# A graph-attention layer on one core: the row fetches of the sync engine leave, every tile is gathered, and more of the gathers wait for TensorE

## The chip, the cores and the metric

The kernel runs on one core of one Trainium2 chip. The metric is device time in microseconds (us): lower is better. A core has TensorE (PE in the profile, with its weight loads as PEld), VectorE (DVE), ScalarE (ACT), GpSimd (POOL) and the sync engine (SP), each with an instruction queue of its own, and 16 DMA engines that move data between HBM and the on-chip memory. The time before is 2110.27 us, the median of three runs (2109.47 to 2112.22).

## The reference

One graph-attention layer with a batch norm and a layer norm, on 12,500 nodes of 128 features (8 heads of 16) and 212,500 edges that are sorted by their target node:

```python
Q, K, V = (x @ WQ), (x @ WK), (x @ WV)            # each (N, 8, 16)
Eh = (edge_attr @ WE)                             # (E, 8, 16)
score = exp(clip((K[src] * Q[dst] / sqrt(16) * Eh).sum(-1), -5, 5))
wV = segment_sum(V[src] * score, dst)
Z  = segment_sum(score, dst)
h  = x + wV / (Z + 1e-6)
h  = (h - mean(h)) * rsqrt(var(h) + 1e-5) * gamma + beta    # over the nodes
out = layernorm(x + h)                                      # over the features
```

What matters here is `K[src]` and `V[src]`: for each edge a row of 256 floats (K and V side by side, 1 KB) has to come from a table, at an index that is data.

## The kernel before, in words

**Tiles and groups.** The edges are cut into T = 1661 tiles of 128. Four tiles make a unit (`U`; the last two units have 3 and 2), and two units make a group (`G` = 8 tiles; the last has 5), so there are NG = 208 groups. A unit's targets lie in a window of 64 nodes.

**The prelude.** It projects x with WK and WV (`table_rows`, L674) and writes the table `kvd` (12,500 rows of 1 KB) to HBM. Meanwhile GpSimd gathers rows of x itself for the first 8 groups (`nxg`), 64 tiles; their K and V are projected from those (`project`, L330), three groups in the prelude and five in the first iterations of the loop. `load_rest` (L166) issues loads from ACT's queue, among them two of `row_ids`, the indices for the row fetches below. `place(runs[0])` (L375) runs in the prelude too; the later runs are placed from iteration 20 on. `place` turns the targets' places within their window (`rel`) by TensorE and writes them as bf16 rows to `relT` in HBM, from where `load_rel` (L400, one group) and `load_quad` (L389, four groups) bring them back, broadcast over 64 partitions. `turned_onehot` (L532) compares them with the partition number.

**The loop.** Iteration g (L793) works on several groups at once, a stage apart. On TensorE, in this order: `add_x(g-3)` (L658), `q_mm(g+3)` (L544, matmul L546), `gather_sum(g-1)` (L629, matmuls L636), `turn_back(g+1)` (L580, L586) and `ehqe(g+2)` (L560, L565 and L573). On VectorE: `products(g)` (L591, K times the turned Q·E, L597), `both(g+1)` (L575), `scores(g)` (L603), small steps, `message(g)` (V times the weight, L621) and `onehot(g+1)`.

**The gathers.** From group 8 on, K and V of a group come by indirect DMAs that GpSimd issues, one of 128 rows for each tile (`gather`, L229, the instruction at L230), into one of nine slots of 8 tiles (slots 0 to 7, and slot 8 from the end of iteration 6). `message(g)` frees the slot of its group; `load_kv` (L284) then puts the gathers of the next group that has none into the list `queued`, and iteration g+1 issues them. From group 17 on, the slot that `message(g)` frees goes to group g+9. `pace(step)` (L241) makes the first gather of the list wait for a TensorE instruction, here `q_mm(g+3)`, from iteration 12 on; `issue()` sends the others without such a wait.

**The rows by the sync engine.** For every eighth group from 18 on (24 groups, `row_plan`, L58), the last tile isn't gathered. SP reads 16 indices in each iteration from 8 on and issues a DMA of one row of 1 KB for each (`fetch_rows`, L273, the DMA at L282), 3072 in all, into the tile `byrow`. So the table's gathers are 1573. In those groups `parts` (L270) splits the second `products` and the `message` in two, one piece for the fetched tile.

**The end.** After the last group come the batch norm's sums, the layer norm of 25 blocks and the output.

Of the kernel before, what the change touches and what calls it, by code (L numbers as in the profile page):

```python
# [9 lines left out]
BF16 = mybir.dt.bfloat16  # L10
U8 = mybir.dt.uint8
I32 = mybir.dt.int32
# [17 lines left out]
ROWS = P  # L30
FIRST_ROW = 8
ROW_LAG = 3
ROW_STREAMS = (("SP", 16),)
RQ = 4
# [22 lines left out]

def row_plan(sizes):  # L58


    full = sizes.count(U) // 2
    used, plan_ = set(), []
    for _, n in ROW_STREAMS:
        groups, end = [], 0
        while True:
            end += P
            g = FIRST_ROW + -(-end // n) - 1 + ROW_LAG
            while g in used:
                g += 1
            if g >= full:  # L70
                break
            used.add(g)
            groups.append(g)
        plan_.append(groups)
    return plan_


def row_groups(sizes):
    return [2 * g for groups in row_plan(sizes) for g in groups]


@with_exitstack
def gnn_kernel(
# [42 lines left out]
    kvd = dram.tile([N, 2 * P], F32, name="kvd")  # L126
    relT = dram.tile([T, P], BF16, name="relT")

# [37 lines left out]
    def load_rest():  # L166
        nc.scalar.dma_start(base_i, bass.AP(tensor=dstb.tensor, offset=dstb.offset, ap=[[0, P], [1, NW]]))
        nc.scalar.dma_start(rel_i[:, :cut], dst[:, :cut])
        for q, m, c, n, at in row_loads:
            nc.scalar.dma_start(row_ids[q % P:q % P + m, c:c + n], bass.AP(  # L170
                tensor=rsrc.tensor, offset=rsrc.offset + at, ap=[[n, m], [1, n]]))
        nc.scalar.dma_start(w_q, wq)
        nc.scalar.dma_start(w_e, we)
        nc.scalar.dma_start(srcs[:, nxg * G:cut], src[:, nxg * G:cut])
# [48 lines left out]
    def kv_view(g, t):  # L223
        SLOT[g] = t[0]
        v = t[1].rearrange("p (g d) -> p g d", d=2 * P)
        KV[g] = lambda a, b, c, n=P: (v[:, a:b, c:c + n] if g not in by_row or b < G else
                                      by_row[g][:, :, c:c + n])

# [20 lines left out]

    by_row, fill = {}, {}  # L250
    row_loads = []
    cols = ids = 0
    for (_, n), groups in zip(ROW_STREAMS, row_plan(usizes)):
        tot = len(groups) * P
        for q in range(-(-tot // n)):
            at = (q % P, cols + q // P * n, min(n, tot - q * n))
            fill.setdefault(FIRST_ROW + q, []).append(at + (groups, q * n))
        for q in range(0, tot // n, P):
            row_loads.append((q, min(P, tot // n - q), cols + q // P * n, n, ids + q * n))
        if tot % n:  # L260
            q = tot // n
            row_loads.append((q, 1, cols + q // P * n, tot % n, ids + q * n))
        cols += -(-tot // (P * n)) * n
        ids += tot
        by_row.update({g: None for g in groups})
    row_ids = consts.tile([P, cols], I32, name="row_ids")
    nc.vector.memset(row_ids, 0)
    kvb = kvd.bitcast(U8).rearrange("n d -> (n d)")

    def parts(g, a, b):  # L270
        return [(a, b - 1), (b - 1, b)] if g in by_row and b == G else [(a, b)]

    def fetch_rows(g):  # L273
        for p, c, n, groups, at in fill.get(g, []):
            _, offs = nc.values_load_multi_w_load_instructions(
                row_ids[p:p + 1, c:c + n], engines=(ET.SP,), min_val=0, max_val=(N - 1) * 8 * P,
                skip_runtime_bounds_check_because="node ids")
            for r, off in enumerate(offs, at):
                k = groups[r // P]
                if r % P == 0:  # L280
                    by_row[k] = late[0].tile([P, 1, 2 * P], F32, name="byrow", bufs=2)
                nc.sync.dma_start(by_row[k][r % P:r % P + 1, 0, :].bitcast(U8), kvb[ds(off, 8 * P)].unsqueeze(0))  # L282

    def load_kv():  # L284
        while free and pending and table[0]:
            g = pending.pop(0)
            i = free.pop(0)
            kv_view(g, (i, slot(i)))
            for j in range(sizes[g] - (g in by_row)):
                queued.append((gather, KV[g](j, j + 1, 0, 2 * P).rearrange("p a d -> p (a d)"), kvd,  # L290
                               starts[g] + j))
            if not steady[0]:
                issue()
# [81 lines left out]
    def place(r):  # L375
        nc.vector.tensor_copy(vw(rel, r), vw(rel_i, r))
        nc.vector.tensor_tensor(vw(rel, r), vw(rel, r), bc(base_f, r), op=OP.subtract)
        end = ustarts[r[0]] + (r[1] - r[0]) * r[2]
        for t in range(ustarts[r[0]], end, P):
            n = min(P, end - t)  # L380
            ps = spare_ps
            nc.tensor.transpose(ps[:n], rel[:, t:t + n], ident)
            row = wp.tile([P, P], BF16, name="relrow", bufs=2)
            nc.vector.tensor_copy(row[:n], ps[:n])
            nc.scalar.dma_start(relT[t:t + n, :], row[:n])

    RB = {}

    def load_quad(q):  # L389
        t = late[0].tile([P, RQ, U * P], BF16, name="rbq", bufs=2)  # L390
        for h in (0, 1):
            at = ustarts[2 * RQ * q + h] * P
            nc.sync.dma_start(t[h * WN:(h + 1) * WN], bass.AP(
                tensor=relT.tensor, offset=relT.offset + at, ap=[[0, WN], [G * P, RQ], [1, U * P]]))
        for k in range(RQ):
            RB[RQ * q + k] = t[:, k, :]

    quads = range(-(-2 * FIRST_ROW // RQ), sizes.count(G) // RQ)

    def load_rel(g):  # L400
# [3 lines left out]
        for h in (0, 1):  # L404
            t, n = ustarts[2 * g + h], usizes[2 * g + h]
            nc.sync.dma_start(RB[g][h * WN:(h + 1) * WN, :n * P],
                              bass.AP(tensor=relT.tensor, offset=relT.offset + t * P, ap=[[0, WN], [1, n * P]]))

# [151 lines left out]
    def ehqe(g):  # L560

        QE[g], WT[g] = [], []
        for a, b in halves(g):
            eh = psp.tile([P, U * P], F32, name="ps_e", bufs=2)[:, :(b - a) * P]
            nc.tensor.matmul(eh, w_e, EA[g][:, a:b, :].rearrange("p a b -> p (a b)"), start=True, stop=True)  # L565
            t = wp.tile([P, U * P], F32, name="wt", bufs=2)
# [3 lines left out]
        for k in range(3):  # L570
            for h, (a, b) in enumerate(halves(g)):
                r = slice(h * WN, (h + 1) * WN)
                nc.tensor.matmul(QE[g][h], Q3[g][r, k, :], OT[g][r, :(b - a) * P], start=(k == 0), stop=(k == 2))  # L573

    def both(g, h):  # L575
# [4 lines left out]
    def turn_back(g):  # L580

        PW[g] = []
        for h, (a, b) in enumerate(halves(g)):
            ps = turned()
            for j in range(b - a):
                nc.tensor.transpose(ps[:, j, :], WT[g][h][:, j * P:(j + 1) * P], ident)  # L586
            PW[g].append(ps)

    PR, SS, RZ = {}, {}, {}

    def products(g, hs=(0, 1)):  # L591
        if 0 in hs:
            PR[g] = wp.tile([P, G, P], F32, name="p", bufs=1)
        for i in hs:
            a, b = halves(g)[i]
            for c, d in parts(g, a, b):
                nc.vector.tensor_tensor(PR[g][:, c:d, :], KV[g](c, d, 0), PW[g][i][:, c - a:d - a, :], op=OP.mult)  # L597

# [16 lines left out]
    def message(g, h=None):  # L615
        if h is not None:
            ranges = parts(g, *halves(g)[h])
        else:
            ranges = halves(g) if g < nxg and g not in SLOT else parts(g, 0, sizes[g])
        for a, b in ranges:  # L620
# [8 lines left out]
    def gather_sum(g):  # L629
# [3 lines left out]
        for j in [*range(n - 1), *range(n, nt(g)), n - 1]:  # L633
            if g and j == n - 1:
                nc.tensor.matmul(AGG[g][0:1, :], carry[WN:, g - 1:g], OS[g - 1][WN:], start=False, stop=False)
            nc.tensor.matmul(AGG[g][WN if j >= n else 0:], OH[g][j], MSG[g][:, j, :], start=(j == 0),  # L636
                             stop=(j == n - 1))

# [154 lines left out]
    for g in range(NG - 2):  # L793
        within(load, g + 4)
        within(load_rel, g + 5)
        if (g + 6) % RQ == 0 and (g + 6) // RQ in quads:
            load_quad((g + 6) // RQ)
        fetch_rows(g)
        within(products, g)
        within(both_halves, g + 1)  # L800
        step = within(add_x, g - 3)
        step = within(q_mm, g + 3) or step
        if step is not None and queued and g >= FIRST_ROW + 4:
            pace(step)
        issue()
        within(gather_sum, g - 1)
        if g + 1 < nxg and g + 1 not in SLOT:
            for _ in project_main(g + 1):
                pass
        within(turn_back, g + 1)  # L810
        within(scores, g)
# [9 lines left out]
        within(turned_onehot, g + 3)  # L821
        within(ehqe, g + 2)
        within(q_mid, g + 3)
# [11 lines left out]
        if g == NG - 5:  # L835
            assert done >= set(range(NPRE))
            norm_first()
        if g == 4:
            nc.vector.tensor_scalar(row_ids, row_ids, 8 * P, None, op0=OP.mult)
        if g == FIRST_ROW - 1:  # L840
            tps.close()
            late.append(tps.enter_context(tc.tile_pool(name="late", bufs=1)))
        if g == FIRST_ROW - 2:
            free.append(NSLOT)
            load_kv()
    last = NG - 1
    g = last - 1
    assert not any(k >= g for k in fill)
    within_checks(g)
# [324 lines left out]
```

## Time and profile before

| what | before |
|---|---|
| median of three runs | 2110.27 us |
| the profiled execution, its time | 2108.13 us |
| its span (first to last instruction) | 2106.3 us |
| granted TensorE clock, mean | 0.925 |
| busy: PE, DVE, POOL, ACT | 1692.8, 1633.1, 1579.5, 635.8 us |
| gathers from the table, from x | 1573, 64 |
| row fetches by SP | 3072 of 1 KB |

How to read it: busy is the time in which an engine executes; an engine whose busy share is under 100% can still be the limit, if something fixed stands between its instructions. "Idle before" is the gap ahead of an instruction, and the name behind the arrow is what ended it; "issue" is a gap for which the profile shows no releaser. A line such as `942/946/1153` gives the shortest, the median and the longest duration in ns.

### The profile page before, as it was taken

To read this page: it belongs to the slowest core of one execution; us is meant where nothing else is said; L and a number is where in the kernel's file an instruction comes from. 1 tells how busy PE (TensorE), PEld (TensorE's weight loads), DVE (VectorE), ACT (ScalarE), POOL (GpSimd) and SP (SyncE) were. 2 spreads that over 40 slices of the span, in tenths; PEclk is the share of its full clock that TensorE was granted. 3 is DMA by queue.
4 is the path that set the end of the run, shared out by engine and by line. 5 is a ranking of instruction groups with operands and counts; after the bars stand their busy time and mean duration, and the time that the engine had idled before them with its cause. 6 is when DMAs were issued, how large, how long until landed. Compare 5 with 4: busy or idle time off the path is not lost.

```text
span 2106.3 us, 37679 instructions
## 1 busy us (share of the span) xinstructions
PE 1692.8 (80%) x9414; PEld 1106.6 (53%) x9414; DVE 1633.1 (78%) x3601; ACT 635.8 (30%) x2480; POOL 1579.5 (75%) x1673
## 2 busy tenths in 40 slices
PE   8899888888777787777778778777777777787777
PEld 6665555555455455445455555554454544454457
DVE  3559989988777778787778787778777778777787
ACT  2353333333222222222222223222222223223225
POOL 7777777777777777777777777777777777777775
PEclk9999989999999999899998898899999999899999
DMA  8956656666566555566565566665566565565684
GB/s 284 306 183 187 188 174 192 188 188 190 166 188 187 175 169 166 159 187 187 177 176 159 165 182 187 178 177 158 168 188 177 177 176 158 166 187 149 181 269 129
DMA packets 177913, 386.83 MB, mean 184 GB/s; under 512 B 38862, under 2 KB 94711, under 8 KB 177687
## 3 DMA queue, kind: packets, MB, share of 16 engines
q0 software_dynamic: 77552, 210.48, 34.1%
q1 hardware_dynamic: 95972, 171.08, 26.7%
q10 hardware_dynamic: 4163, 2.79, 0.4%
q8 instruction: 77, 1.26, 0.2%
q14 instruction: 149, 1.22, 0.2%
HBM read 364.58 MB, written 19.63 MB: 182 GB/s over the span
## 4 chain that ended last, share of the span: by engine, by line
DVE 23%; POOL 22%; DMA 21%; issue 16%; PE 13%; SPq 2%; ACT 2%; DVEq 1%; ACTq 0%; POOLq 0%
POOL slot L230 22%; DMA slot<-kvd,srcs 15%; DVE wt L578 6%; DVE msg L621 4%; DVE s L603 3%; DMA rbq<-relT 3%; PE ps_a L636 3%; PE ps_e L565 2%; DVE p L597 2%; DVE oh L526 2%; DMA ea<-eaT 2%; SPq L282 1%; PE ps_t L586 1%; DVE ot L536 1%; PE ps_m L661 1%
## 5 line engine op out<-in xcount | busy, mean ns | idle before, releaser
L230 POOL DMA_INDIRECT slot<-kvd,srcs x1573 | 1491.0, 948 | 480.5 <-issue 415.2
L636 PE MATMUL ps_a<-msg,oh 128*128 128x136 f32 (+1 forms) x3322 | 555.9, 309 | 0.5 <-DVE msg L621 0.5
L597 DVE TENSOR_TENSOR p<-slot,ps_t 128x512 f32<-128x512 f32 (+1 forms) x410 | 269.2, 672 | 309.8 <-DMA slot<-kvd,srcs 254.2
L636 PEld LDWEIGHTS ps_a<-msg,oh 128*128 128x128 f32 (+1 forms) x3322 | 450.0, 178 | 84.1 <-issue 60.7
L565 PE MATMUL ps_e<-ea,w_e 128*128 128x512 f32 x832 | 438.1, 653 | 32.3 <-DMA ea<-eaT 30.7
L612 ACT ACTIVATE ps_m<-s 128x64 f32<-128x64 f32 (+1 forms) x209 | 47.5, 227 | 1226.0 <-DVE s L611 920.2
L586 PE MATMUL ps_t<-ident,wt 128*128 128x128 f32 x1661 | 249.5, 293 | 113.1 <-DVE wt L578 111.4
L578 DVE TENSOR_TENSOR wt<-wt,ps_q 128x512 f32<-128x512 f32 x416 | 265.6, 680 | 13.0 <-PE ps_q L573 12.5
L661 PE MATMUL ps_m<-ident,at 128*128 128x128 f32 x412 | 99.0, 324 | 218.3 <-DVE oh L529 214.5
L586 PEld LDWEIGHTS ps_t<-ident,wt 128*128 128x128 f32 x1661 | 197.1, 148 | 141.9 <-DVE wt L578 135.3
L567 ACT ACTIVATE wt<-ps_e 128x512 f32<-128x512 f32 x416 | 233.9, 586 | 71.8 <-PE ps_e L565 67.7
L603 DVE TENSOR_REDUCE s<-p 128x64 f32<-128x1024 f32 (+1 forms) x209 | 251.9, 1205 | 0.1
L621 DVE TENSOR_TENSOR msg<-slot,ps_m 128x1024 f32<-128x1024 f32 (+2 forms) x209 | 244.7, 1173 | 1.0 <-ACT ps_m L612 0.7
L565 PEld LDWEIGHTS ps_e<-ea,w_e 128*128 128x128 f32 x832 | 158.3, 212 | 154.4 <-issue 115.8
L661 PEld LDWEIGHTS ps_m<-ident,at 128*128 128x128 f32 x412 | 64.5, 197 | 310.1 <-ACT q L555 283.8
L573 PE MATMUL ps_q<-ot,q 64*128 64x512 bf16 x1248 | 173.1, 384 | 0.0
L573 PEld LDWEIGHTS <-q 64*128 64x128 bf16 x1248 | 44.3, 95 | 195.7 <-issue 171.8
L526 DVE TENSOR_TENSOR oh<-ps_m,rel_i 128x512 f32<-128x512 f32 x208 | 142.0, 683 | 0.0
L515 ACT ACTIVATE xw<-hx 128x64 f32 x416 | 83.9, 248 | 65.2 <-issue 53.0
L652 DVE SCALAR_TENSOR_TENSOR at<-os,keep,rz 128x128 f32<-128x128 f32 x208 | 73.2, 352 | 26.2 <-PE ps_m L661 1.5
L666 ACT ACTIVATE hx<-ps_m 128x64 f32 x412 | 90.4, 219 | 7.9 <-PE ps_m L662 1.2
L546 PE MATMUL ps_m<-w_q,xw 128*128 128x128 f32 x416 | 85.9, 290 | 3.2 <-DVE oh L529 2.8
(173 smaller groups left out, 1549.5 us busy)
## 6 DMA issues: line engine op xcount, KB each, us to landing
ea<-eaT SPq DMA_DIRECT2D x207, 512.0 KB
byrow<-kvd SPq DMA_DIRECT2D x3072, 1.0 KB
slot<-kvd,srcs POOLq DMA_INDIRECT x1573
rbq<-relT SPq DMA_DIRECT2D x94, 256.0 KB
kvd<-slot SPq DMA_DIRECT2D x12, 512.0 KB
kvd<-t SPq DMA_DIRECT2D x12, 512.0 KB
slot<-xT SPq DMA_DIRECT2D x24, 256.0 KB
out<-o SPq DMA_DIRECT2D x23, 256.0 KB
```

What stands on the lines that cost most here:

```text
L230: return nc.gpsimd.indirect_dma_start(out=out, out_offset=None, in_=table, in_offset=bass.IndirectOffsetOnAxis(ap=srcs[:, e:e + 1], axis=0))
L526: nc.vector.tensor_tensor(one, iota_ps[:, None, :].to_broadcast([P, n, P]), r[:, :n, None].to_broadcast([P, n, P]), op=OP.is_equal)
L565: nc.tensor.matmul(eh, w_e, EA[g][:, a:b, :].rearrange("p a b -> p (a b)"), start=True, stop=True)
L567: nc.scalar.activation(t[:, :(b - a) * P], eh, AF.Copy)
L573: nc.tensor.matmul(QE[g][h], Q3[g][r, k, :], OT[g][r, :(b - a) * P], start=(k == 0), stop=(k == 2))
L578: nc.vector.tensor_tensor(t, t, QE[g][h], op=OP.mult)
L586: nc.tensor.transpose(ps[:, j, :], WT[g][h][:, j * P:(j + 1) * P], ident)
L597: nc.vector.tensor_tensor(PR[g][:, c:d, :], KV[g](c, d, 0), PW[g][i][:, c - a:d - a, :], op=OP.mult)
L603: nc.vector.tensor_reduce(SS[g][:, a:b, :], PR[g][:, a:b, :].rearrange("p t (h d) -> p t h d", d=DH), axis=AX.X, op=OP.add)
L621: nc.vector.tensor_tensor(MSG[g][:, a:b, :P].rearrange("p t (h d) -> p t h d", d=DH), KV[g](a, b, P).rearrange("p t (h d) -> p t h d", d=D ...
L636: nc.tensor.matmul(AGG[g][WN if j >= n else 0:], OH[g][j], MSG[g][:, j, :], start=(j == 0), stop=(j == n - 1))
L661: nc.tensor.matmul(ps, AT[g], ident, start=True, stop=False)
```

## The change

It takes out `row_plan`, `fetch_rows`, `row_ids`, `by_row` and `parts`: no row is fetched by SP, and every group from 8 on has all its tiles gathered, 1597 from the table (1661 with those of x). `row_groups` stays as a stub. The constant `FIRST_ROW` becomes `LATE`, with the same value 8.

From iteration 4 on (where the list isn't empty), gathers 1, 4, 6 and 8 of a slot wait for steps of TensorE: for `q_mm(g+3)`, the last matmul of `gather_sum(g-1)`, the last transpose of `turn_back(g+1)` and the last L565 matmul of `ehqe(g+2)`. The gathers between are issued behind them.

`relT` becomes two tensors, one for the even and one for the odd units, so that the places of four groups lie in one run of 4 KB for `load_quad` (before: four runs of 1 KB). For that, `place` copies the even and the odd units of 32 units together into a tile (`stage`) before it turns them: two copies of 128x64 on VectorE more for each turn, and two writes to `relT` where there was one.

```diff
-ROW_STREAMS = (("SP", 16),)
...
-    relT = dram.tile([T, P], BF16, name="relT")
+    at_half, half_rows = [], [0, 0]
+    for w, k in enumerate(usizes):
+        at_half.append(half_rows[w % 2])
+        half_rows[w % 2] += k
+    relT = [dram.tile([n, P], BF16, name=f"relT{h}") for h, n in enumerate(half_rows)]
...
-        for q, m, c, n, at in row_loads:
-            nc.scalar.dma_start(row_ids[q % P:q % P + m, c:c + n], bass.AP(
-                tensor=rsrc.tensor, offset=rsrc.offset + at, ap=[[n, m], [1, n]]))
...
+    def paced(step):
+        if queued and step is not None:
+            pace(step)
+            issue(max(0, len(queued) - 1))
...
-            for j in range(sizes[g] - (g in by_row)):
+            for j in range(sizes[g]):
...
+        k = r[2]
+        for w in range(r[0], r[1], P // (2 * k) * 2):
+            z = min(w + P // (2 * k) * 2, r[1])
+            stage = wp.tile([P, 4, P], F32, name="xt", bufs=2)[:, 0, :]
+            spans, n = [], 0
+            for v in range(w, min(w + 2, z)):
+                c = len(range(v, z, 2))
+                nc.vector.tensor_copy(stage[:, n:n + c * k].rearrange("p (g k) -> p g k", k=k),
+                                      vw(rel, r)[:, v - r[0]:z - r[0]:2, :])
+                spans.append((v, n, c * k))
+                n += c * k
             ps = spare_ps
-            nc.tensor.transpose(ps[:n], rel[:, t:t + n], ident)
+            nc.tensor.transpose(ps[:n], stage[:, :n], ident)
...
-            nc.scalar.dma_start(relT[t:t + n, :], row[:n])
+            for v, a, m in spans:
+                nc.scalar.dma_start(relT[v % 2][at_half[v]:at_half[v] + m, :], row[a:a + m])
...
-                tensor=relT.tensor, offset=relT.offset + at, ap=[[0, WN], [G * P, RQ], [1, U * P]]))
+                tensor=relT[h].tensor, offset=relT[h].offset + at_half[2 * RQ * q + h] * P,
+                ap=[[0, WN], [1, RQ * U * P]]))
...
-        fetch_rows(g)
         within(products, g)
         within(both_halves, g + 1)
         step = within(add_x, g - 3)
         step = within(q_mm, g + 3) or step
-        if step is not None and queued and g >= FIRST_ROW + 4:
+        fine = step is not None and queued and g >= 4
+        if fine:
             pace(step)
-        issue()
-        within(gather_sum, g - 1)
+        issue(max(0, len(queued) - 2) if fine else 0)
+        step = within(gather_sum, g - 1)
+        if fine:
+            paced(step)
...
-        within(turn_back, g + 1)
+        step = within(turn_back, g + 1)
+        if fine:
+            paced(step)
...
-        within(ehqe, g + 2)
+        step = within(ehqe, g + 2)
+        if fine:
+            paced(step)
+        issue()
```

More of the change, by code (lines that the diff above doesn't have):

```diff
@@ L10 @@
 BF16 = mybir.dt.bfloat16
-U8 = mybir.dt.uint8
 I32 = mybir.dt.int32
@@ L30 @@
 ROWS = P
-FIRST_ROW = 8
-ROW_LAG = 3
-ROW_STREAMS = (("SP", 16),)
+LATE = 8
 RQ = 4
@@ L55, in plan @@
     return sizes, starts, cuts, due, thr
[L58 to L75, printed above, removed]
 def row_groups(sizes):
-    return [2 * g for groups in row_plan(sizes) for g in groups]
+    return [0]
 @with_exitstack
@@ L225, in kv_view @@
         v = t[1].rearrange("p (g d) -> p g d", d=2 * P)
-        KV[g] = lambda a, b, c, n=P: (v[:, a:b, c:c + n] if g not in by_row or b < G else
-                                      by_row[g][:, :, c:c + n])
+        KV[g] = lambda a, b, c, n=P: v[:, a:b, c:c + n]
     def gather(out, table, e):
@@ L246, in pace @@
                               reason="pace")
[L250 to L282, printed above, removed]
+    def paced(step):
+        if queued and step is not None:
+            pace(step)
+            issue(max(0, len(queued) - 1))
     def load_kv():
@@ L377, in place @@
         nc.vector.tensor_tensor(vw(rel, r), vw(rel, r), bc(base_f, r), op=OP.subtract)
-        end = ustarts[r[0]] + (r[1] - r[0]) * r[2]
-        for t in range(ustarts[r[0]], end, P):
-            n = min(P, end - t)
+        k = r[2]
[9 more added lines that the diff above has]
+                n += c * k
             ps = spare_ps
-            nc.tensor.transpose(ps[:n], rel[:, t:t + n], ident)
+            nc.tensor.transpose(ps[:n], stage[:, :n], ident)
             row = wp.tile([P, P], BF16, name="relrow", bufs=2)
             nc.vector.tensor_copy(row[:n], ps[:n])
-            nc.scalar.dma_start(relT[t:t + n, :], row[:n])
+            for v, a, m in spans:
+                nc.scalar.dma_start(relT[v % 2][at_half[v]:at_half[v] + m, :], row[a:a + m])
     RB = {}
@@ L391, in load_quad @@
         for h in (0, 1):
-            at = ustarts[2 * RQ * q + h] * P
-            nc.sync.dma_start(t[h * WN:(h + 1) * WN], bass.AP(
-                tensor=relT.tensor, offset=relT.offset + at, ap=[[0, WN], [G * P, RQ], [1, U * P]]))
+            nc.sync.dma_start(t[h * WN:(h + 1) * WN].rearrange("p k d -> p (k d)"), bass.AP(
+                tensor=relT[h].tensor, offset=relT[h].offset + at_half[2 * RQ * q + h] * P,
+                ap=[[0, WN], [1, RQ * U * P]]))
         for k in range(RQ):
             RB[RQ * q + k] = t[:, k, :]
-    quads = range(-(-2 * FIRST_ROW // RQ), sizes.count(G) // RQ)
+    quads = range(-(-2 * LATE // RQ), sizes.count(G) // RQ)
     def load_rel(g):
@@ L404, in load_rel @@
         for h in (0, 1):
-            t, n = ustarts[2 * g + h], usizes[2 * g + h]
-            nc.sync.dma_start(RB[g][h * WN:(h + 1) * WN, :n * P],
-                              bass.AP(tensor=relT.tensor, offset=relT.offset + t * P, ap=[[0, WN], [1, n * P]]))
+            n = usizes[2 * g + h]
+            nc.sync.dma_start(RB[g][h * WN:(h + 1) * WN, :n * P], bass.AP(
+                tensor=relT[h].tensor, offset=relT[h].offset + at_half[2 * g + h] * P, ap=[[0, WN], [1, n * P]]))
     mv = consts.tile([P, 2], F32, name="mv")
@@ L564, in ehqe @@
             eh = psp.tile([P, U * P], F32, name="ps_e", bufs=2)[:, :(b - a) * P]
-            nc.tensor.matmul(eh, w_e, EA[g][:, a:b, :].rearrange("p a b -> p (a b)"), start=True, stop=True)
+            step = nc.tensor.matmul(eh, w_e, EA[g][:, a:b, :].rearrange("p a b -> p (a b)"), start=True, stop=True)
             t = wp.tile([P, U * P], F32, name="wt", bufs=2)
@@ L573, in ehqe @@
                 nc.tensor.matmul(QE[g][h], Q3[g][r, k, :], OT[g][r, :(b - a) * P], start=(k == 0), stop=(k == 2))
+        return step
     def both(g, h):
@@ L585, in turn_back @@
             for j in range(b - a):
-                nc.tensor.transpose(ps[:, j, :], WT[g][h][:, j * P:(j + 1) * P], ident)
+                step = nc.tensor.transpose(ps[:, j, :], WT[g][h][:, j * P:(j + 1) * P], ident)
             PW[g].append(ps)
+        return step
     PR, SS, RZ = {}, {}, {}
@@ L595, in products @@
             a, b = halves(g)[i]
-            for c, d in parts(g, a, b):
-                nc.vector.tensor_tensor(PR[g][:, c:d, :], KV[g](c, d, 0), PW[g][i][:, c - a:d - a, :], op=OP.mult)
+            nc.vector.tensor_tensor(PR[g][:, a:b, :], KV[g](a, b, 0), PW[g][i][:, :b - a, :], op=OP.mult)
     def scores(g, h=None):
@@ L616, in message @@
         if h is not None:
-            ranges = parts(g, *halves(g)[h])
+            ranges = [halves(g)[h]]
         else:
-            ranges = halves(g) if g < nxg and g not in SLOT else parts(g, 0, sizes[g])
+            ranges = halves(g) if g < nxg and g not in SLOT else [(0, sizes[g])]
         for a, b in ranges:
@@ L635, in gather_sum @@
                 nc.tensor.matmul(AGG[g][0:1, :], carry[WN:, g - 1:g], OS[g - 1][WN:], start=False, stop=False)
-            nc.tensor.matmul(AGG[g][WN if j >= n else 0:], OH[g][j], MSG[g][:, j, :], start=(j == 0),
-                             stop=(j == n - 1))
+            step = nc.tensor.matmul(AGG[g][WN if j >= n else 0:], OH[g][j], MSG[g][:, j, :], start=(j == 0),
+                                    stop=(j == n - 1))
+        return step
     def sums_out(g):
@@ L837, in gnn_kernel @@
             norm_first()
-        if g == 4:
-            nc.vector.tensor_scalar(row_ids, row_ids, 8 * P, None, op0=OP.mult)
-        if g == FIRST_ROW - 1:
+        if g == LATE - 1:
             tps.close()
             late.append(tps.enter_context(tc.tile_pool(name="late", bufs=1)))
-        if g == FIRST_ROW - 2:
+        if g == LATE - 2:
             free.append(NSLOT)
@@ L847, in gnn_kernel @@
     g = last - 1
-    assert not any(k >= g for k in fill)
     within_checks(g)
```

## Prediction

> **What bounds the kernel now.** I read the page's busy rows first, then its groups and chain, then the gathers' own line, the waits, and two stretches of the timeline. From the page:
>
> ```profile
> span 2106.3 us, 37679 instructions
> ...
> PE 1692.8 (80%) x9414; PEld 1106.6 (53%) x9414; DVE 1633.1 (78%) x3601; ACT 635.8 (30%) x2480; POOL 1579.5 (75%) x1673
> ...
> DVE 23%; POOL 22%; DMA 21%; issue 16%; PE 13%; SPq 2%; ACT 2%; DVEq 1%; ACTq 0%; POOLq 0%
> ...
> L230 POOL DMA_INDIRECT slot<-kvd,srcs x1573 | 1491.0, 948 | 480.5 <-issue 415.2
> ```
>
> No engine is over 80% busy, and the chain is shared by everybody, so the page names no bound at first sight. But POOL's gathers have 1491.0 us of execution and 480.5 us of idle time before them: 1971.5 us, 94% of the span, and nearly all of that idle time has no releaser ("issue"). The view of line 230 and POOL's list of waits (waited for, us in total, times, longest) show what the idle time is:
>
> ```profile
> L230 POOL DMA_INDIRECT slot<-kvd,srcs x1573: 942/946/1153, 83.8 to 2053.5; - x197
> L230 POOLq EVENT_SEMAPHORE  x227: 17/43/6137, 11.2 to 2042.4; - x114
> L230 POOL DMA_INDIRECT slot<-x,srcs x64: 940/944/1152, 3.1 to 82.0; - x64
> ```
>
> ```profile
> POOL slot L230 <- issue: 431.3, 1415, 0.3
> ...
> POOL slot L230 <- PE ps_m L546: 9.1, 30, 0.3
> ...
> POOL slot L230 <- DVE msg L621: 2.9, 8, 0.8
> ```
>
> A gather takes 0.946 us, and 0.30 us pass before the next, whether it waited for something or not. From 83.8 to 2053.5 us that is one gather each 1969.7 / 1572 = 1.253 us without a break; the 64 gathers of x fill 3.1 to 82.9 us at the same step. So **POOL's issue of gathers is the bound from the first microsecond to 2054.5**, and 52 us of tail follow. VectorE shows the other side: `products` waited for a gather's landing 100 times, 254.2 us in all. The loop could run faster: before iteration 20, when gathers are in hand, it needs 7.5 us for an iteration, while eight gathers need 10.0.
>
> **The gathers.** 24 more from the table (1597 for 1573), each 1.253 us on the engine that never pauses: **+30.1 us**. I count no part of it as hidden, since no gap in POOL's stream is longer than 0.8 us. What SP stops doing is worth nothing by itself: its 3072 issues of 0.23 us lie beside the gathers, and `products` waited for a fetched row only 3 times, 8.2 us, in iterations that wait for gathers anyway. The 24 split pieces of `products` and `message` (0.28 us each) leave VectorE, which has slack. A lighter DMA load could only shorten landings, and the landing of one gather lies beside the issue of the next; only the last one's counts.
>
> **The waits.** A paced gather stops POOL, and every later gather queues behind it. Whether it stops depends on how far POOL lags behind the steps. For the slot that `message(g-1)` frees the steps are those of iteration g, and its gathers feed group g+8. In the steady part POOL gathers for group g+1 or g+2 while iteration g runs (`products` waits for the landing), so a step of iteration g is some 65 us old when its gather comes up. In the first iterations the lag is small. Groups 8 to 16 are 72 gathers, up to the one at 172.89; the first of group 17 came at 174.71 (start, us, engine):
>
> ```profile
> 172.76 0.35 DVE L536 TENSOR_SCALAR ot<-rb,wiota 128x512 bf16<-128x512 bf16 x1
> ...
> 172.89 1.04 POOL L230 DMA_INDIRECT slot<-kvd,srcs  x1 [0.30 <-issue]
> ...
> 173.23 1.21 DVE L621 TENSOR_TENSOR msg<-slot,ps_m 128x1024 f32<-128x1024 f32 x1
> ...
> 174.71 0.94 POOL L230 DMA_INDIRECT slot<-kvd,srcs  x1 [0.78 <-DVE msg L621]
> ...
> 176.30 0.39 PE L546 MATMUL ps_m<-w_q,xw 128*128 128x128 f32 x2
> ```
>
> It was released by `message(8)`. In the changed kernel it also waits for `q_mm(12)`, the L546 pair that ends at 176.69: **+2.0 us**, once, for all that follows. Its other steps are then on time: the matmuls of `gather_sum(8)` end at 179.2, the transposes at 180.1, L565 at 181.8, and gathers 4, 6 and 8 would come at 180.5, 183.0 and 185.5. Group 18's first step ends at 184.3 against 186.7, and from there the loop gains 2.5 us in each iteration. Group 16's four steps (iteration 7, the first with a list to pace) end 2.4 to 6.2 us before its gathers; the groups before it are listed behind the steps and aren't paced. A wait that is already met costs nothing in the trace: the 30 gathers after L546 had the gap of 0.3 us that all have. The bounds of this term are 0 (the loop comes to iteration 9 two microseconds earlier) and +2.8 (0.8 later, next part).
>
> **Prelude and places.** What comes before iteration 9 moves `q_mm(12)`, and with it POOL, one for one. Two ACT issues of `row_ids` go; ACT's queue stood in them and their neighbours:
>
> ```profile
> 11.65 1.00 ACTq L170 DMA_DIRECT2D row_ids<-rsrc  x2
> 12.70 1.29 ACTq L172 DMA_DIRECT2D w_q<-wq  x1
> 14.03 0.47 ACTq L173 DMA_DIRECT2D w_e<-we  x1
> 15.36 0.33 ACTq L174 DMA_DIRECT2D srcs<-src  x1
> 15.73 0.60 ACT L311 ACTIVATE t<-ps_e 128x512 f32<-128x512 f32 x1 [4.94 <-DMA row_ids<-rsrc]
> ```
>
> That gives back 1.0 us, or up to 1.8 if the pause before the last issue (14.50 to 15.36) goes too. Against it `place(runs[0])` gets four copies of 128x64. The chain runs through it (L376, L377, two turns at L382, 33.8 to 35.8 us). The nearest row is the clip of 128x64, L611, 0.195 us: +0.8 us. I take the two as cancelling: **0**, bounds -1.8 and +0.8. The other 24 copies (28 in all) and 13 more small writes come in iterations that wait for gathers. The loads of places in runs of 4 KB (94 loads, the same bytes) have three iterations of time and so no price; before, they had it too.
>
> **A price that the copies could have on POOL itself.** In the fence above the gather at 172.89 took 1.04 us, 0.1 more than the median, behind an L536 of VectorE that began 0.13 us before it. So a VectorE instruction can hold a gather. By this row 28 copies cost between 0 and 28 x 0.2 = 5.6 us; I take 0, because the mean of 1573 gathers is 2 ns over the median with some 200 L536 among them. The Trainium skill's page "SBUF — State Buffer", section "Who interferes with whom", has a rule that speaks against the change: a copy on VectorE in its two-port mode takes the port pair that GpSimd shares, and blocks it for the whole instruction. By that rule each copy could hold a gather for its length, and the sum would be up to 2148; by the row of means it stays at 2142. The trace agrees with the rule in the pair shown.
>
> **The sum.** 30.1 + 2.0 + 0 = +32.1 us. The profiled execution took 2108.13 (1.8 around its span of 2106.3), so its counterpart takes 2140.2. It lies 2.1 below the median of the runs shown; on the median the sum is 2142.4, and I forecast **2142**.
>
> **The rivals.** First, **the held gather becomes a rule.** With eight gathers for each group the loop is in step with POOL at 10.0 us, so an L536 might meet the same spot of a gather in every group. At 0.1 us (the pair shown) for groups 17 to 207 that is 19 us: 2161. For it: the step is fixed. Against it: now seven of eight groups already have eight gathers, and the stretches are 3 us in all. 7%.
>
> Second, **met waits aren't free.** There are 4 x 192 paced gathers (groups 16 to 207) instead of 188, 580 more. If each put a wait instruction into POOL's stream at its own length (17 ns shortest, 43 ns median, row POOLq above), 10 to 25 us: 2152 to 2167. For it: 227 such instructions are there. Against it: no wait on L546 shows a gap over 0.3. 6%.
>
> Third, the other side: **SP's row DMAs slow POOL's issue today**, through the gap of 0.30 us that no releaser explains, and their end gives back more than it costs. At 0.1 us less of that gap the 1597 gathers take 160 us less: about 1983. It decides from 17 ns for each gather (27.9 us / 1661), where the change would come within 0.2% of before. Against it: POOL's busy time and count in four stretches (first without rows, as SP's first row starts at 169.8 us; the other two with them):
>
> ```profile
> 90.00:168.00 78.00, 59.09 (x63) 1.00 0.59 184
> 600.00:678.00 78.00, 59.09 (x63) 0.91 0.63 189
> 1400.00:1478.00 78.00, 59.09 (x63) 0.93 0.56 161
> ```
>
> 63 gathers in each, to the hundredth of a microsecond. 2%, half of it within 0.2%.
>
> **Range and chances.** Forecast 85%, rivals 7, 6 and 2%. Low end: 2142.4 - 2.0 - 1.8 - 3 (no stretches) = 2135.6; high end: 2142.4 + 0.8 + 5.6 = 2148.8. I round to 2135 to 2150, which leaves the rivals out. 0.2% (4.2 us) is about what a measurement of this kernel can tell from no change: slower by more than that 98%, within it 1%, faster 1%.
>
> **What the profile after would show.** 1597 gathers from the table, one each 1.253 us, the last starting at about 2085.6. One gap of 2.5 to 3 us before a gather near 176 us with L546 as its releaser, and no other over 1 us. A mean of 948 ns; 955 or more would be the first rival. A gap of 0.32 us or more in three of eight gathers would be the second. The tail stays at 52 us. The forecast is wrong if POOL pauses in the steady part, or if a gather's step is shorter than 1.24 us.

## The result, and the profile after

The changed kernel takes **2142.89 us** (median of 4 runs, 2141.03 to 2143.92); the kernel before takes 2109.87 (4 runs beside them, 2109.30 to 2112.22). The ratio is 1.0154, 95% interval 1.0141 to 1.0167: 33.0 us more on the medians, where 32.1 were forecast. The profiled execution of the changed kernel is the slowest of its four, 2143.92; its span is 35.4 us longer than that of before. In the changed kernel the gather is L208, `q_mm` L504, `turn_back`'s transpose L545, `ehqe` L523 and L531, `gather_sum` L595, `message` L580.

From the page after (the same rows as those shown of before):

```profile
span 2141.7 us, 31796 instructions
...
PE 1697.2 (79%) x9414; PEld 1108.8 (52%) x9414; DVE 1633.1 (76%) x3579; ACT 635.0 (30%) x2480; POOL 1603.0 (75%) x1697
...
PE 25%; DMA 24%; DVE 23%; issue 13%; POOL 10%; ACT 2%; DVEq 1%; ACTq 0%; SPq 0%; POOLq 0%
...
L208 POOL DMA_INDIRECT slot<-kvd,srcs x1597 | 1514.5, 948 | 491.8 <-issue 352.7
```

Of the busy rows POOL's grew most: 23.5 us, all of it in the gathers' line, which has 11.3 us more of idle time as well. POOL's share of the chain fell from 22% to 10%, though it is the same bound as before. The likely reason is that more gaps now have a semaphore event near them, which the chain takes for their cause; so these shares don't tell which engine is the limit. The gathers' own line and POOL's waits do:

```profile
L208 POOL DMA_INDIRECT slot<-kvd,srcs x1597: 940/946/1117, 84.6 to 2088.3; - x200
L208 POOLq EVENT_SEMAPHORE  x803: 17/17/6530, 11.3 to 2080.5; - x161
```

```profile
POOL slot L208 <- issue: 369.5, 1213, 0.3
POOL slot L208 <- PE ps_e L523: 25.6, 84, 0.3
...
POOL slot L208 <- PE ps_t L545: 17.4, 44, 4.3
...
POOL slot L208 <- PE ps_m L504: 17.4, 57, 0.3
```

The last column is the longest wait. 57 gathers stand behind L504 and none waited over 0.3 us; one of the 44 behind L545 waited 4.3. From group 17's first gather, at 178.71 us, to the last, at 2088.29, it is one gather each 1.2530 us (1.2525 before, from 174.71 on). The span's 35.4 us by parts:

| part | forecast | profiled executions |
|---|---|---|
| the first gather of group 17 starts later (174.71, then 178.71) | +2.0 | +4.0 |
| 24 gathers more | +30.1 | +30.1 |
| a longer step of the others after group 17 began | 0 | +0.7 |
| from the last gather's start to the end (52.77, then 53.41) | 0 | +0.6 |

Of the 4.0 us, 0.8 were there before any wait: the table's first gather came at 84.60 us instead of 83.78.

The pause isn't where it was forecast. The timeline of after around 158 and 177 us (start, us, engine):

```profile
153.40 0.94 POOL L208 DMA_INDIRECT slot<-kvd,srcs  x1 [0.30 <-issue]
...
157.70 0.66 PE L545 MATMUL ps_t<-ident,wt 128*128 128x128 f32 x4 [0.21 <-ACT t L260]
...
158.63 0.94 POOL L208 DMA_INDIRECT slot<-kvd,srcs  x1 [4.28 <-PE ps_t L545]
```

```profile
177.01 0.39 PE L504 MATMUL ps_m<-w_q,xw 128*128 128x128 f32 x2
...
177.46 0.95 POOL L208 DMA_INDIRECT slot<-kvd,srcs  x1 [0.30 <-PE ps_m L504]
178.71 0.95 POOL L208 DMA_INDIRECT slot<-kvd,srcs  x1 [0.30 <-issue]
```

The gather at 158.63 is the 57th from the table, the first of **group 15**, and it waits for `turn_back(7)` in iteration 6. The first of group 17 is the one at 178.71. `q_mm(12)` ended at 177.40, before it, so that wait was already met.

Why group 15 waits at all is in a line of the changed loop:

```python
fine = step is not None and queued and g >= 4
...
if fine:
    paced(step)
```

If the list is empty, Python's `and` returns the list itself, not `False`. In iteration 6 it is empty at this line; `project_main(7)` then fills it with group 15's gathers before `turn_back` is reached, and the second test of `fine` finds a list that isn't empty. So "where the list isn't empty", as the change was described, holds only for a list that is filled at this line; a list that is filled later in the iteration is paced from `turn_back` on. The prediction had these groups "listed behind the steps" and so not paced.

The experiments ran in three groups, each on one chip. On the chips of the second and third group the kernel before itself takes 2748.88 and 2750.55 us (medians), against 2110.25 on the first, so every ratio below compares kernels on one chip, and the times of different groups aren't compared.

### The profile page after: what moved, and what is told of

Same layout as the page of the kernel before. It is cut to its first block, busy times and chain, and to the rows that moved or that the text cites. A ratio compares the mean times of both kernels' runs of the same rounds, so it can differ in the third digit from the quotient of the medians.

```text
span 2141.7 us, 31796 instructions
## 1 busy us (share of the span) xinstructions
PE 1697.2 (79%) x9414; PEld 1108.8 (52%) x9414; DVE 1633.1 (76%) x3579; ACT 635.0 (30%) x2480; POOL 1603.0 (75%) x1697
## 3 DMA queue, kind: packets, MB, share of 16 engines
q8 instruction: 77, 1.26, 0.2%
## 4 chain that ended last, share of the span: by engine, by line
PE 25%; DMA 24%; DVE 23%; issue 13%; POOL 10%; ACT 2%; DVEq 1%; ACTq 0%; SPq 0%; POOLq 0%
DMA slot<-kvd,srcs 24%; POOL slot L208 10%; DVE wt L537 6%; PE ps_a L595 6%; PE ps_e L523 6%; PE ps_t L545 5%; DVE s L562 4%; DVE msg L580 4%; DVE oh L484 2%; DVE p L556 2%; PE ps_m L621 1%; DVE oh L487 1%; DVE ot L494 1%; PE ps_t L283 1%; PE ps_a L594 1%
## 5 line engine op out<-in xcount | busy, mean ns | idle before, releaser
L208 POOL DMA_INDIRECT slot<-kvd,srcs x1597 | 1514.5, 948 | 491.8 <-issue 352.7
L595 PE MATMUL ps_a<-msg,oh 128*128 128x136 f32 (+1 forms) x3322 | 551.2, 307 | 1.0 <-DVE msg L580 1.0
L556 DVE TENSOR_TENSOR p<-slot,ps_t 128x512 f32<-128x512 f32 x410 | 272.6, 680 | 363.3 <-DMA slot<-kvd,srcs 345.8
L595 PEld LDWEIGHTS ps_a<-msg,oh 128*128 128x128 f32 (+1 forms) x3322 | 446.3, 177 | 85.5 <-issue 61.2
L523 PE MATMUL ps_e<-ea,w_e 128*128 128x512 f32 x832 | 438.6, 654 | 0.7 <-ACT wt L525 0.7
L545 PE MATMUL ps_t<-ident,wt 128*128 128x128 f32 x1661 | 260.8, 301 | 160.8 <-DVE wt L537 158.4
L545 PEld LDWEIGHTS ps_t<-ident,wt 128*128 128x128 f32 x1661 | 203.7, 152 | 195.1 <-DVE wt L537 188.9
L580 DVE TENSOR_TENSOR msg<-slot,ps_m 128x1024 f32<-128x1024 f32 (+2 forms) x209 | 248.0, 1188 | 0.4 <-ACT ps_m L571 0.3
L523 PEld LDWEIGHTS ps_e<-ea,w_e 128*128 128x128 f32 x832 | 160.1, 214 | 119.8 <-issue 83.2
L531 PE MATMUL ps_q<-ot,q 64*128 64x512 bf16 x1248 | 172.1, 382 | 0.0
L531 PEld LDWEIGHTS <-q 64*128 64x128 bf16 x1248 | 44.3, 95 | 196.0 <-issue 171.4
L504 PE MATMUL ps_m<-w_q,xw 128*128 128x128 f32 x416 | 86.3, 292 | 3.2 <-DVE oh L487 2.7
```

Of the source, the lines that this page charges most:

```text
L208: return nc.gpsimd.indirect_dma_start(out=out, out_offset=None, in_=table, in_offset=bass.IndirectOffsetOnAxis(ap=srcs[:, e:e + 1], axis=0))
L523: step = nc.tensor.matmul(eh, w_e, EA[g][:, a:b, :].rearrange("p a b -> p (a b)"), start=True, stop=True)
L545: step = nc.tensor.transpose(ps[:, j, :], WT[g][h][:, j * P:(j + 1) * P], ident)
L556: nc.vector.tensor_tensor(PR[g][:, a:b, :], KV[g](a, b, 0), PW[g][i][:, :b - a, :], op=OP.mult)
L580: nc.vector.tensor_tensor(MSG[g][:, a:b, :P].rearrange("p t (h d) -> p t h d", d=DH), KV[g](a, b, P).rearrange("p t (h d) -> p t h d", d=D ...
L595: step = nc.tensor.matmul(AGG[g][WN if j >= n else 0:], OH[g][j], MSG[g][:, j, :], start=(j == 0), stop=(j == n - 1))
```

## The experiments

**First group: the waits.** Kernel before: 2110.25 us (15 runs). *a_one*: the changed kernel with the one wait of before, from iteration 12.

```diff
-        fine = step is not None and queued and g >= 4
+        fine = step is not None and len(queued) > 0 and g >= LATE + 4
...
-        issue(max(0, len(queued) - 2) if fine else 0)
-        step = within(gather_sum, g - 1)
-        if fine:
-            paced(step)
+        issue()
+        within(gather_sum, g - 1)
...
```

> The changed kernel with the waits of the kernel before: only the first gather of a slot waits, and only from iteration 12 on. Theory (POOL's count of gathers, and one hold of POOL before group 17's first gather): that gather is released by message(8) at about 175.4 us instead of by q_mm(12) at 177.46, so 2.0 us under the changed kernel, about 30.1 + 0.7 = 30.8 us over the kernel before. Rival (met waits cost something each): 10 to 25 us under the changed kernel, since 580 waits go.

Measured: 2140.06 us, ratio 1.0141 (1.0126 to 1.0157), +29.8 us. The first gather of group 15 starts at 153.56 and that of group 17 at 174.78, as in before (154.02 and 174.71); the last one at 2083.51, 29.98 us after that of before: 24 x 1.2525 = 30.1.

```profile
174.78 0.94 POOL L208 DMA_INDIRECT slot<-kvd,srcs  x1 [1.51 <-DVE msg L580]
```

What follows: gathers, prelude, places and the end of SP's rows come to 29.8 together (26.6 to 33.1 by the interval), so the last three add up to nothing that shows.

*a_four12*: the four waits, but from iteration 12.

```diff
-        fine = step is not None and queued and g >= 4
+        fine = step is not None and len(queued) > 0 and g >= LATE + 4
```

> The changed kernel with all four waits of a slot, but from iteration 12 on instead of 4. Theory: the four waits of later slots are all met, so the same as with one wait, within 0.5 us: about 30.8 us over the kernel before, and the rate of the gathers 1.2525 to 1.254 us. Rival (met waits cost): as the changed kernel, and over the kernel with one wait by 10 us or more.

Measured: 2139.77 us, 1.0141 (1.0125 to 1.0157), 0.3 us less than a_one. The groups view of a_one, then of a_four12:

```profile
L208 POOL DMA_INDIRECT slot<-kvd,srcs x1597 | 1513.5, 948 | 487.8 <-issue 429.9 <-DVE p L556 13.7 <-DVE wt L537 10.4
```

```profile
L208 POOL DMA_INDIRECT slot<-kvd,srcs x1597 | 1514.7, 948 | 486.5 <-issue 354.6 <-PE ps_e L523 25.0 <-DMA slot<-kvd,srcs 20.4
```

75 us moved from "issue" to other names, while the sum of the idle time stayed. That is the pattern of a wait that is already met: it gives the fixed gap of 0.30 us a name and doesn't lengthen it.

*a_bool*: the changed kernel with a plain truth value in that line.

```diff
-        fine = step is not None and queued and g >= 4
+        fine = step is not None and len(queued) > 0 and g >= 4
```

> The changed kernel, but slots that were not yet in the list when the iteration's first step was made are not paced: group 15's first gather does not wait for turn_back(7) any more. Theory: the pause of 4.3 us at 158.6 us goes, and a pause of some 3 us comes before group 17's first gather, which q_mm(12) releases at the same 177.4 us: the time stays within 0.5 us of the changed kernel. Rival (the pause at 158.6 us is what the waits cost): 2 to 4 us under the changed kernel.

Measured: 2142.70 us, 1.0156 (1.0142 to 1.0170), the changed kernel's time to 0.2 us. The pause at 158 us is gone (group 15 starts at 153.57), and there is one where the prediction had it, before group 17:

```profile
173.88 0.39 PE L504 MATMUL ps_m<-w_q,xw 128*128 128x128 f32 x2
...
174.54 0.94 POOL L208 DMA_INDIRECT slot<-kvd,srcs  x1 [1.26 <-PE ps_m L504]
```

It is 1.26 us long where some 3 were expected, since `q_mm(12)` ended at 174.27 in this execution. So it is shown that the pause of group 15 comes from this line, and that either pause makes the other needless. The size isn't settled. In this execution group 17 began at 174.54 us, no later than in a_one (174.78), so here the early wait cost POOL's stream nothing. Of the 2.2 us between this profiled span (2138.8) and a_one's (2136.6), 0.3 lie in the stream and 1.9 behind the last gather, so a good part of a_bool's distance from a_one is scatter.

*b_four*: the kernel before, rows and places untouched, with the four waits of the changed kernel.

```diff
+    def paced(step):
+        if queued and step is not None:
+            pace(step)
+            issue(max(0, len(queued) - 1))
...
-        if step is not None and queued and g >= FIRST_ROW + 4:
+        fine = step is not None and queued and g >= 4
+        if fine:
...
-        within(turn_back, g + 1)
+        step = within(turn_back, g + 1)
+        if fine:
+            paced(step)
```

> The kernel before with the four waits from iteration 4 on, its rows still fetched by SP and its places unchanged. Theory: only the early hold acts, group 17's first gather moves from 174.7 to 176.75 us: 2.0 us over the kernel before, no other change of POOL's rate. Rival (met waits cost): 10 us or more over the kernel before.

Measured: 2113.22 us (11 runs), 1.0012 (1.0003 to 1.0021): +2.5 us by the ratio, 0.6 to 4.4 (3.0 on the medians). Group 15's first gather waits 5.04 us for `turn_back`, as in the changed kernel:

```profile
159.73 0.94 POOL L230 DMA_INDIRECT slot<-kvd,srcs  x1 [5.04 <-PE ps_t L592]
```

So within this interval the waits cost the same with and without the rows, and the change's 33.0 us are some 30 of gathers and 2.5 to 3 of waits.

**Second and third group: places and rows.** *a_oldplaces* and its repeat *a_oldplaces2*: the changed kernel with one `relT`, runs of 1 KB and no copies. *b_newplaces*: the kernel before with the change's places.

```diff
-    relT = [dram.tile([n, P], BF16, name=f"relT{h}") for h, n in enumerate(half_rows)]
+    relT = dram.tile([T, P], BF16, name="relT")
...
-                nc.vector.tensor_copy(stage[:, n:n + c * k].rearrange("p (g k) -> p g k", k=k),
-                                      vw(rel, r)[:, v - r[0]:z - r[0]:2, :])
```

> The changed kernel with the places of the kernel before: one relT, no copies, one write to relT for each turn, runs of 1 KB. Theory: the places act only through the prelude; iteration 9 comes 0.7 to 2.5 us earlier (the copies and the extra writes of the first run go, and what the two row_ids issues on ACT gave back stays), so 0.7 to 2.5 us under the changed kernel. Rival (the copies hold POOL's gathers, or runs of 4 KB matter in the steady part): more than 3 us under it, or over it.

> The changed kernel with the places of the kernel before (one relT, no copies, one write to relT for each turn, runs of 1 KB); the same kernel again, since the first pair of times came from a chip on which the kernel before itself took 2749 us. Theory: the places act only through the prelude; iteration 9 comes 0.7 to 2.5 us earlier, so 0.7 to 2.5 us under the changed kernel's 2142.9. Rival (the copies hold POOL's gathers, or runs of 4 KB matter in the steady part): more than 3 us under it, or over it.

> The kernel before with the places of the changed kernel, rows and waits as before. Theory: only the prelude moves, by up to 2.5 us: 0.5 to 2.5 us over the kernel before; POOL's rate 1.2525 us. Rival (runs of 4 KB lighten the queues and speed the steady part): under the kernel before.

Measured: 0.9439 (0.9418 to 0.9460) and 0.9448 (0.9425 to 0.9472) for the changed kernel without its places, 1.0015 (0.9995 to 1.0035) for before with them. The second says that the places cost nothing measurable on that chip, within -1.4 and +9.6 us. But on these chips the kernel without rows is 5.5% **faster** than before, the reverse of the first chip. All three expectations rested on POOL as the bound; there it isn't one, and the places by themselves stay unmeasured where before takes 2110.

*b_rows8*, *b_rows8b*, *b_rows20*, *b_rows24*, *b_rows24b*: the kernel before with other numbers of rows for each iteration (a last b marks the repeat on the third chip; b_rows20 ran on the third alone).

```diff
-ROW_STREAMS = (("SP", 16),)
+ROW_STREAMS = (("SP", 8),)      # 20, 24
```

> The kernel before with 8 rows fetched by SP in an iteration instead of 16: 12 groups by rows instead of 24, so 1585 gathers from the table. Theory: +12 x 1.2525 = 15.0 us. Rival (SP's row DMAs slow POOL's issue): less than 10 us over, or under the kernel before.

> The kernel before with 8 rows fetched by SP in an iteration instead of 16: 12 groups by rows, 1585 gathers; again, for the same reason. Theory: +12 x 1.2525 = 15.0 us. Rival (SP's row DMAs slow POOL's issue): less than 10 us over, or under the kernel before.

> The kernel before with 20 rows in an iteration: 30 groups by rows, 1567 gathers. Theory: -6 x 1.2525 = -7.5 us, as SP's 20 x 0.32 = 6.5 us, its index load of 1.4 and its other issues of 0.7 fit into an iteration of 9.8 us. Rival (SP becomes the bound): no gain, with products waiting for rows.

> The kernel before with 24 rows in an iteration: 36 groups by rows, 1561 gathers. Theory, if SP keeps up: 12 gathers fewer, of which group 16's lies before the hold at group 17 and gives nothing, so -11 x 1.2525 = -13.8 us, to about 2096. Rival (SP becomes the bound): 24 rows take 24 x 0.32 = 7.7 us of SP in an iteration of 9.8, and with its index load of 1.4 and its other issues of 0.7 it is full; then rows come late, products waits for them, and the time is that of before or more.

> The kernel before with 24 rows in an iteration: 36 groups by rows, 1561 gathers; again, for the same reason. Theory, if SP keeps up: -11 x 1.2525 = -13.8 us, to about 2096. Rival (SP becomes the bound): SP's 7.7 + 1.4 + 0.7 = 9.8 us fill an iteration of 9.8; rows come late, products waits for them, and the time is that of before or more.

Measured, with the changed kernel without its places as the row for 0 and b_newplaces, from the second chip, as that for 16 (gathers: from the groups view, busy us, mean ns and idle us before them):

| rows in an iteration | ratio (third chip) | gathers: busy, mean; idle | PE waits for `ea`: us |
|---|---|---|---|
| 0 (a_oldplaces2) | 0.945 | 1511.4, 946; 877 | none listed |
| 8 (b_rows8b) | 0.950 | 1506.6, 951; 894 | none listed |
| 16 (b_newplaces) | 1.0015 | 1491.8, 948; 1056 | 430 |
| 20 (b_rows20) | 1.100 | 1486.1, 948; 1313 | 727 |
| 24 (b_rows24b) | 1.212 | 1478.7, 947; 1623 | 1055 |

On the second chip 8 rows gave 0.954 and 24 gave 1.213. So 8 rows took 127 and 140 us less than before, where 15 more were expected, and 20 and 24 rows were slower, as the rival (SP becomes the bound) had it. The groups view of b_newplaces, its list of waits and the view of its row issues:

```profile
L234 POOL DMA_INDIRECT slot<-kvd,srcs x1573 | 1491.8, 948 | 1056.1 <-PE ps_m L559 434.6 <-issue 409.9 <-PE ps_a L649 51.3
```

```profile
PE ps_e L578 <- DMA ea<-eaT: 429.5, 125, 11.1
```

```profile
L286 SPq MOVE byrow<-kvd x3072: 2/29/1400, 247.1 to 2667.3; - x192
L286 SPq DMA_DIRECT2D byrow<-kvd x3072: 2/227/1445, 247.2 to 2667.4; - x192
```

The same of before, on the first chip:

```profile
PE ps_e L565 <- DMA ea<-eaT: 30.7, 15, 4.5
```

```profile
L282 SPq MOVE byrow<-kvd x3072: 29/29/38, 169.8 to 1998.6; - x192
L282 SPq DMA_DIRECT2D byrow<-kvd x3072: 217/228/347, 169.9 to 1998.7; - x192
```

A gather takes the 948 ns that it takes elsewhere, but POOL stands idle 576 us longer than in before on the first chip, most of it in paced gathers that wait for L559 (`q_mm`). L578 (`ehqe`) waits 429.5 us for `ea`, the edge features, whose loads SP issues behind its rows. On the first chip, in before, that wait is 30.7 us. One row's issue takes up to 1.4 us here and at most 0.35 there; the median is the same. A plain register move (`MOVE`) of the same line also takes up to 1.4 us here, 0.04 there, so it isn't the row DMAs alone that are slow on SP. The wait for `ea` grows with the rows, from 430 to 727 and 1055 us, and so does the time. From this it is inferred, not shown, that on these chips **SP's queue** sets the loop's step where there are 16 rows or more; POOL's idle time shows that POOL doesn't. What slows SP's instructions the traces don't show.

## Why the prediction was right, point by point

**The bound and the gathers: right.** 24 gathers more at 1.253 us. a_one, in which little else of the change is left, put the last gather 29.98 us later, and its step was 1.2524 us.

**The waits: the sum nearly right, the place wrong.** The step that failed is "the groups before it are listed behind the steps and aren't paced". It was read from the order of the loop, without the value of `fine`. The pause came two groups earlier and was 4.3 us long instead of 2.5 to 3, and group 17 moved by 4.0 us instead of 2.0 (0.8 of it from before the waits); on the medians the early waits cost 2.8 (2142.89 - 2140.06) to 3.1 (2142.89 - 2139.77), and 2.5 in b_four. The price came out near because the same thing was priced: POOL runs ahead of the loop once in the first iterations, and the first wait that stops it makes the next one needless.

**Met waits are free: right**, and this rejects the second rival. a_four12 has the four waits on every slot from iteration 12 and lies 0.3 us from a_one, where the rival had 10 to 25.

**Prelude and places, 0: nothing in the runs speaks against it, and alone they weren't measured on the first chip.** ACT's evacuation came at 13.94 us instead of 15.73, all of the 1.8 us by which this term could have lowered the time. They were lost again, to the four writes of `place` to `relT` on ACT and their landing. The timeline of after:

```profile
13.94 0.60 ACT L260 ACTIVATE t<-ps_e 128x512 f32<-128x512 f32 x1 [3.38 <-PE ps_q L641]
...
33.78 2.44 ACTq L343 DMA_DIRECT2D relT<-relrow  x4
...
37.44 0.40 ACT L473 ACTIVATE xw<-hx 128x64 f32 x2 [8.07 <-DMA relT<-relrow]
```

`xw` starts at 37.44 us, against 37.55 before. The first table gather came between 83.39 and 85.01 us in six profiled executions (before 83.78, after 84.60, and the four of the first group), a scatter larger than the term. a_one, which has the new places, leaves room for -3.5 to +3.0 for this term and the end of the rows together (26.6 and 33.1, less 30.1).

**The copies on POOL: 0.5 us of the bound of 5.6.** One of three gathers that a copy held (timeline of after):

```profile
870.04 1.09 POOL L208 DMA_INDIRECT slot<-kvd,srcs  x1 [0.30 <-DMA slot<-kvd,srcs]
870.34 0.29 DVE L334 COPY xt<-rel_i 128x64 f32<-128x64 f32 x2
```

1.09 us for 0.946, 0.15 us more. The three took 1.092, 1.093 and 1.117. All 28 copies ran beside a gather, 15 gathers in all; the other twelve were at most 0.03 us longer than the median. The Trainium skill's page "SBUF — State Buffer", section "Who interferes with whom", says that a copy in VectorE's two-port mode and GpSimd shut each other out of a shared pair of ports, and that the one that is issued first has the pair for its whole instruction. The three long gathers fit this, and so do the copies that took up to 0.43 us (median 0.19); that most pairs cost nothing the rule alone doesn't explain, and no run shows in which mode the copies ran.

**First rival (a held gather becomes a rule): rejected.** 79 gathers took over 0.955 us, 58 before; the mean is 948.3 ns against 947.9.

**Third rival (SP's rows slow POOL's issue): rejected as it was put.** On the first chip the step of the gathers is 1.253 us with and without rows, and on the other two the gather's own time is the same. A gain from fewer rows did come up there, but not through POOL's issue: what shrank with the rows was the wait for the loads behind them on SP's queue.

**The tail**: 52 us were forecast, 53.4 came; 53.1, 53.6 and 55.0 in a_one, a_four12 and a_bool. It is scatter of this size that makes 2142.89 and the terms' sum agree to a microsecond partly by luck.

## What to carry to other kernels

If an engine issues at a fixed step without a pause, the price of work that moves onto it is the count times the step, and what another engine is spared is worth nothing; find the step from first start, last start and count, not from the busy share. A wait costs only where its engine runs ahead of the step that it waits for: look for that in the first iterations, take each condition at its value and not at its intention, and don't add up pauses in one stream, since the first absorbs the next. What limits a kernel can differ from chip to chip, as it did on the three here, so a trade of work between two queues is worth a run on more than one.

## What the runs showed of the hardware that wasn't expected

The same kernel took 2110 us on one chip and 2749 and 2751 on two others, and the trade between SP and POOL changed its sign: without rows it is 1.5% slower on the first, and (with the old places) 5.5% faster on the others. Each chip had one group of runs, so a lasting property of the chip and its state at that time can't be told apart. The granted clock of TensorE was lower as well (0.82 in b_newplaces, 0.925 in before's profiled execution). Part of the 640 us goes with the wait for `ea` behind SP's rows. But the kernel without rows takes 2594 and 2598 us there too, against 2143 on the first chip, with no wait of TensorE for `ea` listed. The lower clock is one candidate: TensorE's busy time is 1858.2 us in a_oldplaces2 and 1697.2 in the changed kernel on the first chip. No run separates it, and it doesn't cover stretches such as this one of a_oldplaces2, in which none of PE, DVE, ACT and POOL executes anything from 1510.96 to 1512.02 us and then three start within a quarter of a microsecond:

```profile
1509.93 0.82 PE L518 MATMUL ps_q<-ot,q 64*128 64x512 bf16 x6
1510.01 0.95 POOL L204 DMA_INDIRECT slot<-kvd,srcs  x1 [0.30 <-issue]
1512.02 0.28 ACT L588 ACTIVATE os<-ps_a 128x136 f32<-128x136 f32 x1 [4.94 <-PE ps_q L518]
1512.02 0.69 DVE L471 TENSOR_TENSOR oh<-ps_m,rel_i 128x512 f32<-128x512 f32 x1 [3.38 <-PE ps_q L518]
1512.26 0.94 POOL L204 DMA_INDIRECT slot<-kvd,srcs  x1 [1.30 <-PE ps_q L518]
```

All three are put down to L518, whose group had started at 1509.93 with 0.82 us of work, so by the trace, where the ends of matmuls are modelled, the work named had ended 1.3 us before they started. The granted clock around it (1507.2 to 1513.8) reads 1.00. Added up over the trace, the stretches of over 0.5 us in which none of PE, DVE, ACT and POOL executes come to 190 us in a_oldplaces2, 138 of them; in before and after there is none. There is another sign: for many waits of a_oldplaces2 the profile names no releaser in this core's trace ("remote", 420.5 us in ACT's largest group and 237.4 before gathers), and none of before or after is of that kind. What delays these instructions the traces don't show, and the cause stays open. Open too: whether a number of rows above 16 would beat 2110 on the first chip, where POOL is the bound; those runs fell on chips where it isn't.
